# Four runs of edges per partition instead of eight, in a graph-network and mixture-of-experts kernel

## The chip, the cores and the metric

The kernel runs on one core of one Trainium2 chip. The metric is device time in microseconds (us), the median of several executions. A profile is one further execution, recorded instruction by instruction. The core's engines are TensorE (PE, with its weight loads PEld), VectorE (DVE), ScalarE (ACT), GpSimd (POOL) and SyncE (SP); each works through its own instructions in order, and they wait for one another by semaphores. Sixteen DMA engines move data between the main memory and the on-chip memory of 128 partitions; here nearly all transfers are issued from SP's queue, and gathers and scatters by index from POOL's.

## The reference

There are 6250 nodes of 256 features and 100,000 edges of 96 features. The edges are sorted by `dst`, and most go to nodes of low number.

```python
dst = jnp.minimum((6250 * uniform ** 2.0).astype(jnp.int32), 49999)   # then sorted, src with it

# graph layer, on layernorm(x); col = dst
out1 = segment_sum(edge_attr, col, n)
cnt  = segment_sum(ones, col, n)
out2 = where(cnt > 0, segment_max(edge_attr, col, n), 0)
out3 = out1 / maximum(cnt, 1)
h = concatenate([x, out1, out2, out3, u[batch]], axis=1)              # 256 + 3*96 + 64
h = relu(h @ W1 + b1) @ W2 + b2                                       # hidden 1024
x = x + (h + layernorm_x)

# mixture of 16 experts, best 2 of each node, on layernorm(x)
logits = x @ gate_w + gate_b;  w, idx = top 2, softmax of the two
moe = sum_k w_k * (relu(x @ w1[idx_k] + b1) @ w2[idx_k] + b2)         # 256 -> 512 -> 256
x = x + layernorm(x + moe) * gamma + beta
```

All numbers are fp32.

## The kernel before, in words

**Two stages.** The first makes the sums, maxima and means of the edges of each node, runs the graph layer's two products, chooses the experts and scatters the rows to the experts' lists in main memory. The second takes those lists in blocks of 256 rows (`run_block`, PE lines L1166 and L1190), and joins, normalizes and writes the result. The change lies in the first stage.

**Nodes.** A tile is 125 nodes (`P`), a group (`GRP`) has four tiles, the first group two. There are 13 groups, taken from the last nodes to the first, so that nodes with few edges come first. For a group, `hidden` (L772, L789) and `output` (L800) are PE's products, `turn` (L763) its transposes. `residual` (L805 to L810), `stats_x` (L690), `add_b2` (L724), `choose`, `rank` and `place` (L845 to L895) are DVE's work; `send` (L899) scatters the rows.

**Edges of groups 0 and 1.** Each node's few edges lie in a window of 20 edges, which is gathered, masked, summed and maximized (`cut_window` to `mask_window`, L572 to L612). `mask_window` adds a `base`, which is zero unless the input does not fit the kernel's assumptions. Then a fallback, behind a branch, computes everything more slowly.

**Edges of the other groups.** The 95,000 edges before these lie in seven regions. Region c has 125 partitions with `RR` = 8 runs each, and every run is `JR[c]` consecutive edges: 125 x 8 x (6, 5, 5, 10, 21, 20, 28). Regions 0 to 6 serve 1, 1, 1, 2, 3, 2 and 1 groups (`GR`). Within a region the kernel goes over the positions of the runs from the last to the first, all 125 x 8 runs at once. A position's row is the running sum and the running maximum over the edges of the same node up to the run's end: the row of the position behind it, times `keep` (1 if the next edge has the same node, else 0), plus this edge; and the same with `min` of `bar` and `max`. These are the four instructions of an *edge step*, on 125 partitions x `RR` x 96 elements (L316, L317, L319, L320). The first position of a region is copied by ACT.

Positions go in chunks of up to `JS` = 2. `load_edges` (L176) loads a chunk in two DMAs (80 and 45 partitions, `halves`), with three buffers `raw`; the results go from three buffers `rw` to `rows_d` in main memory (L329), in two DMAs. One contiguous piece is a chunk's positions of one run: 2 x 96 x 4 bytes in, twice that out.

**The carry.** A run's last node may go on in the next run. `chain_runs` handles that at a region's end, in three parts. `over_runs` carries over the runs of a partition (L395, L396: `RR` - 1 pairs of instructions of 96 elements into `ct`). `over_partitions` carries over partitions, after PE's transposes. `to_runs` (L436, L438) spreads the carry to all runs with four instructions of `RR` x 96 elements and stores `ct` to `carry_d` by POOL (L440). `ct` has one buffer. `take_edges` (L730) and `take_carry` (L737) gather, for each node, its row and the carry of the next run; `join_edges` (L743, L745) combines them.

**The order of work** is written by a planner when the kernel is built. A group has 12 slots; every task is put into a slot with a cost in microseconds. The edge steps are a stream (`edge_stream`): in each slot it is advanced until a credit of `SLOT` = 4.6, less the costs of the other tasks, is used up. A stream item's cost is the number after `yield`. Before a group's `take_edges`, `edges_until(c)` advances the stream to the end of that region, whatever the credit:

```python
            if fn is take_edges:
                edges_until(args[0])
            fn(*args)
            credit -= cost
```

The last region is needed at slot 134 (`B - 10` of group 12).

Of the kernel before, what the change touches and what calls it, by code (L numbers as in the profile page):

```python
# [18 lines left out]

P = 125  # L20
PA = 80
RR = 8
GW = 2
WE = 20
WB = 5
JR = (6, 5, 5, 10, 21, 20, 28)
GR = (1, 1, 1, 2, 3, 2, 1)
JS = 2
JB = 3
KB = 250  # L30
GS = 4
# [14 lines left out]
def kernel(  # L46
# [18 lines left out]
    nc = tc.nc  # L65
    N, D = x.shape
    E, EF = edge.shape
# [3 lines left out]
    NT = N // P  # L71
# [27 lines left out]
    rows_d = dram.tile([ER, 2 * EF], F32, name="rows_d")  # L99
# [199 lines left out]
    def steps():  # L299

        for i, (c, s, n) in enumerate(chunks):
            e0, J = REG[c]
            if s + n == J:
                mark_runs(c)
                yield 1.5, False, None
            raw, prev = raws.pop(i), prevs.pop(c, None)
            rw = EP_["rw"].tile([P, RR, JS, 2 * EF], F32, name="rw")
            bcast = [P, RR, EF]
            for j in reversed(range(n)):
                x_j, su, mx = raw[:, :, j, :], rw[:, :, j, 0:EF], rw[:, :, j, EF:]  # L310
                if prev is None:
                    nc.scalar.copy(su, x_j)
                    nc.scalar.copy(mx, x_j)
                    prev = x_j, x_j
                else:
                    nc.vector.tensor_tensor(su, prev[0], keep[c][:, :, s + j, None].to_broadcast(bcast), op=OP.mult)  # L316
                    nc.vector.tensor_tensor(mx, prev[1], bar[c][:, :, s + j, None].to_broadcast(bcast), op=OP.min)  # L317
                    yield 1.9, False, None
                    nc.vector.tensor_tensor(su, su, x_j, op=OP.add)  # L319
                    nc.vector.tensor_tensor(mx, mx, x_j, op=OP.max)  # L320
                    prev = su, mx
                    if j:
                        yield 1.9, True, None
            prevs[c] = prev
            if i + JB < len(chunks):
                load_edges(i + JB)
            to = rows_of(c).rearrange("(p r j) f -> p r j f", p=P, j=J)
            for o, i_ in halves(to[:, :, s:s + n], rw[:, :, :n]):
                nc.sync.dma_start(o.rearrange("p r j f -> p r (j f)"), i_.rearrange("p r j f -> p r (j f)"))  # L329
            yield 1.9, True, c if s == 0 else None  # L330

    clock = [-1]
    told = [-1]
# [43 lines left out]

    def chain_runs(c):
        prev = prevs.pop(c)
        ct = chp.tile([P, RR, 2 * EF], F32, name="ct")  # L380
        kb, kp, kb2 = (chp.tile([P, RR], F32, name=nm) for nm in ("kbar", "kp", "kbar2"))

        def over_runs():
# [9 lines left out]
            for r in reversed(range(RR - 1)):  # L393
                to = ct[:, r, 0:EF], ct[:, r, EF:]
                nc.vector.scalar_tensor_tensor(to[0], run[0], kall[:, c, r:r + 1], prev[0][:, r, :], op0=OP.mult, op1=OP.add)  # L395
                nc.vector.scalar_tensor_tensor(to[1], run[1], kb[:, r:r + 1], prev[1][:, r, :], op0=OP.min, op1=OP.max)  # L396
# [35 lines left out]
        def to_runs():  # L432
            tmp = chp.tile([P, RR, EF], F32, name="tmp")
            for h, k, o0, o1 in ((0, kp, OP.mult, OP.add), (1, kb2, OP.min, OP.max)):
# [1 line left out]
                nc.vector.tensor_tensor(tmp, over_runs.pc[:, None, h * EF:(h + 1) * EF].to_broadcast([P, RR, EF]),  # L436
                                        k[:, :, None].to_broadcast([P, RR, EF]), op=o0)
                nc.vector.tensor_tensor(cs, cs, tmp, op=o1)  # L438
# [929 lines left out]
    def windows_of(t, n):  # L1368
# [28 lines left out]
    with tc.If(bad_v != 0):  # L1397

        NC = (KC + 1) * GS * P - 1
        space = chp.tile([P, RR, EF], F32, name="tmp").rearrange("p r f -> p (r f)")  # L1400
        et, ob = space[:, 0:EF + 1], space[:, P:P + 2 * (EF + 1)].rearrange("p (h f) -> p h f", h=2)
        far, df = space[0:1, P:2 * P], space[0:1, 3 * P:4 * P]
        dt_ = space[0:1, 4 * P:5 * P].bitcast(I32)
        dst_v = dst.rearrange("(a b) -> a b", b=P)
        for lo in range(0, N, NC):
            sums = [wk.tile([128, KC + 1, GS * P], F32, name="inT").rearrange("p k n -> p (k n)")[:EF + 1] for _ in range(2)]
# [17 lines left out]
            for n0 in range(0, min(NC, N - lo), P):  # L1424
# [11 lines left out]
        nc.sync.dma_start(base[0], rows_d[W0 * P:NT * P].rearrange("(i p) f -> p i f", p=P))  # L1436
        nc.vector.tensor_scalar(nw, cnt_f[:, W0:], 1.0, None, op0=OP.min)
        for t in range(NT - W0):
            nc.vector.tensor_scalar(base[0][:, t, :], base[0][:, t, :], nw[:, t:t + 1], None, op0=OP.mult)
    with tc.manual_schedule():  # L1440
        global_part()
        stats_x(0, 0)
# [124 lines left out]
```

## Time and profile before

| what | value |
|---|---|
| time, median of 3 runs (lowest to highest) | 1291.13 us (1291.03 to 1294.33) |
| the profiled execution's own time | 1299.43 us |
| its span, mean granted TensorE clock | 1297.6 us, 0.955 |
| busy: PE, PEld | 1113.4 us (86%), 783.4 us (60%) |
| busy: DVE, ACT, POOL | 963.4 us (74%), 612.6 us (47%), 558.8 us (43%) |
| edge steps, DVE: L316, L317, L319, L320 | 352 instructions of 125x768, 948 to 955 ns each |
| to runs, DVE: L436, L438 | 28 instructions of 125x768, 949 to 961 ns each |
| over runs, DVE: L395, L396 | 98 instructions of 125x96, 310 to 318 ns each |
| moved by DMA | 261.25 MB in 179475 packets |

The span runs from the first instruction to the last; the execution's own time has 1.8 us beside it. Busy shares are means over both stages. In the slices of the profile, each engine has one digit per fortieth of the span, its busy share in tenths. Lines with stretches give the busy microseconds of each engine in a stretch, with the number of instructions, then the granted clock, the mean busy share of the 16 DMA engines and what they moved. A line of a wait names who waited, for whom, how long in all, how often, and the longest. A timeline line gives start, duration, engine, line, operation and shapes.

### The profile page before, as it was taken

How to read it: one execution, taken by the hardware profiler on the slowest of the kernel's cores; microseconds unless marked ns; L12 is line 12 of the kernel's file. 1: busy time of each engine (PE TensorE's matmuls, PEld its weight loads, DVE VectorE, ACT ScalarE, POOL GpSimd, SP SyncE). 2: the span in 40 equal slices, each digit the busy share in tenths (PEclk: the TensorE clock that was granted, in tenths of full speed). 3: DMA queues.
4: the chain of work that ended last, by engine and by line, in shares of the span. 5: the costliest groups of instructions: out<-in, count | busy, mean ns of one | idle time of the engine just before them, and what ended most of it. 6: DMA issues, size and time to landing. Idle time of an engine off the chain costs nothing.

```text
span 1297.6 us, 16883 instructions
## 1 busy us (share of the span) xinstructions
PE 1113.4 (86%) x4637; PEld 783.4 (60%) x4637; DVE 963.4 (74%) x2754; ACT 612.6 (47%) x1449; POOL 558.8 (43%) x721
## 2 busy tenths in 40 slices
PE   2484796998789989899989999998999998989992
PEld 1252363655455554646646566886888777778881
DVE  4569787988988979999989422444377777778885
ACT  3484253662437542343424422432466666656662
POOL 4121142663347645375263333030145554545664
PEclk9897898999889998999999999998999999999996
DMA  5948785797779998898997331231677777778972
GB/s 163 209 108 234 206 242 160 204 242 208 216 222 267 252 244 228 235 255 228 274 260 237 90 95 42 66 100 50 195 229 228 231 238 252 254 228 254 280 259 73
DMA packets 179475, 261.25 MB, mean 201 GB/s; under 512 B 35915, under 2 KB 145963, under 8 KB 173729
## 3 DMA queue, kind: packets, MB, share of 16 engines
q1 hardware_dynamic: 140241, 202.23, 54.4%
q0 software_dynamic: 39008, 57.35, 16.1%
q8 instruction: 40, 0.66, 0.2%
q14 instruction: 74, 0.61, 0.2%
q10 hardware_dynamic: 112, 0.41, 0.1%
HBM read 146.70 MB, written 122.01 MB: 207 GB/s over the span
## 4 chain that ended last, share of the span: by engine, by line
PE 35%; DVE 13%; ACT 3%; DMA 3%; issue 3%; POOL 1%; POOLq 0%; SPq 0%; ACTq 0%; DVEq 0%
PE acc L1190 14%; PE acc L1166 11%; PE acc L772 5%; PE acc L800 3%; DVE yb L1089 2%; ACT yb L1091 2%; DVE rw L320 1%; DVE rw L317 1%; DVE rw L319 1%; DVE rw L316 1%; DMA xt<-in_x_dram 1%; ACT hb L1172 1%; DMA cg<-carry_d,next_i 1%; DMA xg_d<-xt,pos_i 1%; POOL xg_d L899 1%
## 5 line engine op out<-in xcount | busy, mean ns | idle before, releaser
L772 PE MATMUL acc<-inT,w1x 128*128 128x500 f32 (+1 forms) x832 | 369.0, 592 | 8.9 <-DVE xt L805 8.9
L772 PEld LDWEIGHTS acc<-inT,w1x 128*128 128x128 f32 x832 | 159.0, 199 | 169.7 <-issue 151.9
L1166 PE MATMUL acc<-xT,wt 128*128 128x256 f32 x912 | 223.2, 388 | 29.3 <-ACT hb L1172 25.7
L899 POOL DMA_INDIRECT xg_d<-xt,pos_i x100 | 134.4, 1344 | 250.2 <-DVE xt L895 119.8
L1190 PE MATMUL acc<-wt,hb 128*128 128x256 f32 x912 | 207.1, 380 | 0.0
L1166 PEld LDWEIGHTS acc<-xT,wt 128*128 128x128 f32 x912 | 169.2, 191 | 62.3 <-ACT hb L1172 38.1
L1190 PEld LDWEIGHTS acc<-wt,hb 128*128 128x128 f32 x912 | 174.1, 191 | 23.9
L800 PE MATMUL acc<-w2s,hT 128*125 128x256 f32 x800 | 186.5, 388 | 0.0
L800 PEld LDWEIGHTS acc<-w2s,hT 128*125 128x125 f32 x800 | 150.5, 193 | 23.7 <-issue 1.9
L1102 POOL DMA_INDIRECT g<-y_d,from_i x86 | 91.8, 1067 | 120.8 <-DMA y_d<-yb 90.5
L1135 POOL DMA_INDIRECT out_dram<-g,to_i x86 | 89.1, 1036 | 102.7 <-ACT hb L1172 86.5
L1091 ACT ACTIVATE yb<-yb,w_b 128x256 f32<-128x256 f32 x114 | 51.7, 501 | 154.0 <-DVE yb L1089 147.8
L495 POOL DMA_INDIRECT gb<-in_dst_dram,blk_i x50 | 74.1, 1483 | 114.2 <-issue 59.4
L1172 ACT ACTIVATE hb<-acc,wt 128x256 f32<-128x256 f32 x200 | 87.7, 464 | 49.5 <-PE acc L1166 41.0
L1089 DVE TENSOR_TENSOR yb<-acc,xe 128x512 f32<-128x512 f32 x57 | 39.4, 691 | 88.3 <-PE acc L1190 57.4
L794 ACT ACTIVATE hT<-acc,c 128x500 f32<-128x500 f32 (+1 forms) x104 | 60.1, 660 | 71.4 <-PE acc L789 71.4
L319 DVE TENSOR_TENSOR rw<-rw,raw 125x768 f32<-125x768 f32 x88 | 83.8, 953 | 0.0
L320 DVE TENSOR_TENSOR rw<-rw,raw 125x768 f32<-125x768 f32 x88 | 83.7, 951 | 0.0
L316 DVE TENSOR_TENSOR rw<-rw,keep 125x768 f32<-125x768 f32 x81 | 76.8, 948 | 5.0 <-DMA rows_d<-rw 4.9
L317 DVE TENSOR_TENSOR rw<-rw,bar 125x768 f32<-125x768 f32 x81 | 77.0, 950 | 0.0
L730 POOL DMA_INDIRECT at<-rows_d,first_i x44 | 61.6, 1399 | 34.2 <-issue 21.5
L737 POOL DMA_INDIRECT cg<-carry_d,next_i x44 | 63.2, 1437 | 25.7 <-issue 11.3
(313 smaller groups left out, 1577.9 us busy)
## 6 DMA issues: line engine op xcount, KB each, us to landing
wt<-in_wpack_dram SPq DMA_DIRECT2D x44, 1026.0 KB
rows_d<-rw SPq DMA_DIRECT2D x46, 960.0 KB
rows_d<-rw SPq DMA_DIRECT2D x46, 540.0 KB
raw<-in_edge_dram SPq DMA_DIRECT2D x46, 480.0 KB
xb<-xg_d SPq DMA_DIRECT2D x57, 263.0 KB
y_d<-yb SPq DMA_DIRECT2D x57, 256.0 KB
raw<-in_edge_dram SPq DMA_DIRECT2D x46, 270.0 KB
xt<-in_x_dram SPq DMA_DIRECT2D x12, 500.0 KB
```

The source lines that it names most:

```text
L316: nc.vector.tensor_tensor(su, prev[0], keep[c][:, :, s + j, None].to_broadcast(bcast), op=OP.mult)
L317: nc.vector.tensor_tensor(mx, prev[1], bar[c][:, :, s + j, None].to_broadcast(bcast), op=OP.min)
L319: nc.vector.tensor_tensor(su, su, x_j, op=OP.add)
L320: nc.vector.tensor_tensor(mx, mx, x_j, op=OP.max)
L772: nc.tensor.matmul(G[g]["pH"][m % 4][:, :n * P], w1x[:, k, m * 128:(m + 1) * 128], inT[:, k, :n * P], start=(k == 0), stop=False)
L800: nc.tensor.matmul(pO, G[g]["hT"][m][:, i * P:(i + 1) * P], w2s[:, m, :], start=(m == 0), stop=(m == HC - 1))
L899: d = nc.gpsimd.indirect_dma_start(out=xg_d[:, :], out_offset=IndirectOffsetOnAxis(ap=G[g]["pos"][:, i, k:k + 1], axis=0), in_=G[g]["xt"][ ...
L1102: d = nc.gpsimd.indirect_dma_start(out=g[:, h, :].bitcast(I32), out_offset=None, in_=y_d[:, :], in_offset=IndirectOffsetOnAxis(ap=BL[b]["f ...
L1135: d = nc.gpsimd.indirect_dma_start(out=out[:, :], out_offset=IndirectOffsetOnAxis(ap=BL[b]["to"][:, h:h + 1], axis=0), in_=g[:, h, :], in_ ...
L1166: nc.tensor.matmul(pB[i][:, half, :], wt[:, k * FF + m * 128:k * FF + (m + 1) * 128], xT[:, k, :], start=(k == 0), stop=(k == DC - 1))
L1172: nc.scalar.activation(hb[:, m, :], pB[i][:, half, :], AF.Relu, bias=bias)
L1190: nc.tensor.matmul(pY[:, h, :], hb[:, m, h * 128:(h + 1) * 128], wt[:, W2O + m * D:W2O + (m + 1) * D], start=(m == order[0]), stop=(m == o ...
```

## The change

A partition holds four runs per region instead of eight, and `JR` is doubled, so a region holds the same edges. An edge step has 125 x 4 x 96 elements, there are twice as many positions, and a chunk has up to four of them. The planner's costs of an edge step and of the parts of the carry are set anew, and `over_runs` yields once instead of three times. `ct` gets two buffers. Before, the zero `base` of groups 0 and 1 lay in one buffer of `ct`, which is now too small for it: group 1's lies in a buffer of `ct`, group 0's in that of `tmp`. The fallback's scratch moves to buffers of `hT`. The rest of the fallback's edits is left out here.

```diff
-RR = 8
+RR = 4
-JR = (6, 5, 5, 10, 21, 20, 28)
+JR = (12, 10, 10, 20, 42, 40, 56)
-JS = 2
+JS = 4
...
                     nc.vector.tensor_tensor(su, prev[0], keep[c][:, :, s + j, None].to_broadcast(bcast), op=OP.mult)
                     nc.vector.tensor_tensor(mx, prev[1], bar[c][:, :, s + j, None].to_broadcast(bcast), op=OP.min)
-                    yield 1.9, False, None
+                    yield 1.0, False, None
                     nc.vector.tensor_tensor(su, su, x_j, op=OP.add)
                     nc.vector.tensor_tensor(mx, mx, x_j, op=OP.max)
                     prev = su, mx
                     if j:
-                        yield 1.9, True, None
+                        yield 1.0, True, None
...
-            yield 1.9, True, c if s == 0 else None
+            yield 1.0, True, c if s == 0 else None
...
-        ct = chp.tile([P, RR, 2 * EF], F32, name="ct")
+        ct = chp.tile([P, RR, 2 * EF], F32, name="ct", bufs=2)
...
                 run = to
-                if r % 3 == 0:
-                    yield 1.8
+                if r == 0:
+                    yield 1.6
...
                 nc.vector.tensor_tensor(cs, cs, tmp, op=o1)
-                yield 1.9
+                yield 1.1
...
-        nc.vector.scalar_tensor_tensor(gi, gi, nw[:, j:j + 1], base[0][:, j, :], op0=OP.mult, op1=OP.add)
+        nc.vector.scalar_tensor_tensor(gi, gi, nw[:, j:j + 1], base[1 - g][:, i, :], op0=OP.mult, op1=OP.add)
...
-    base.append(chp.tile([P, RR, 2 * EF], F32, name="ct").rearrange("p r f -> p (r f)")[:, 0:(NT - W0) * 2 * EF]
+    base.append(chp.tile([P, RR, 2 * EF], F32, name="ct", bufs=2)[:, 0:z1 - a1])
+    base.append(chp.tile([P, RR, EF], F32, name="tmp").rearrange("p r f -> p (r f)")[:, 0:(z - a) * 2 * EF]
                 .rearrange("p (t f) -> p t f", f=2 * EF))
...
-        nc.gpsimd.memset(base[0], 0.0)
+        for t in base:
+            nc.gpsimd.memset(t, 0.0)
...
-        space = chp.tile([P, RR, EF], F32, name="tmp").rearrange("p r f -> p (r f)")
+        space, more = (htp.tile([128, GS * P], F32, name="hT")[:P] for _ in range(2))
...
```

More of the change, by code (lines that the diff above doesn't have):

```diff
@@ L1399 @@
         NC = (KC + 1) * GS * P - 1
-        space = chp.tile([P, RR, EF], F32, name="tmp").rearrange("p r f -> p (r f)")
+        space, more = (htp.tile([128, GS * P], F32, name="hT")[:P] for _ in range(2))
         et, ob = space[:, 0:EF + 1], space[:, P:P + 2 * (EF + 1)].rearrange("p (h f) -> p h f", h=2)
-        far, df = space[0:1, P:2 * P], space[0:1, 3 * P:4 * P]
-        dt_ = space[0:1, 4 * P:5 * P].bitcast(I32)
+        far, df = more[0:1, 0:P], more[0:1, P:2 * P]
+        dt_ = more[0:1, 2 * P:3 * P].bitcast(I32)
         dst_v = dst.rearrange("(a b) -> a b", b=P)
@@ L1435 @@
                     nc.sync.dma_start(cnt_f[q0 - t * P:q1 - t * P, t:t + 1], ob[q0 - lo - n0:q1 - lo - n0, 0, EF:])
-        nc.sync.dma_start(base[0], rows_d[W0 * P:NT * P].rearrange("(i p) f -> p i f", p=P))
+        for t, (t0, t1) in zip(base, ((a1, z1), (a, z))):
+            nc.sync.dma_start(t, rows_d[t0 * P:t1 * P].rearrange("(i p) f -> p i f", p=P))
         nc.vector.tensor_scalar(nw, cnt_f[:, W0:], 1.0, None, op0=OP.min)
         for t in range(NT - W0):
-            nc.vector.tensor_scalar(base[0][:, t, :], base[0][:, t, :], nw[:, t:t + 1], None, op0=OP.mult)
+            to = base[0][:, t, :] if t < z1 - a1 else base[1][:, t - (z1 - a1), :]
+            nc.vector.tensor_scalar(to, to, nw[:, t:t + 1], None, op0=OP.mult)
     with tc.manual_schedule():
```

## The prediction

> **What bounds the kernel now.** I read the page's slices first, then the busy time by stretches of 100 us, then VectorE's waits, SP's waits, and last the timeline for the step from one instruction to the next. Of the slices, the engines and the DMA engines:
>
> ```profile
> PE   2484796998789989899989999998999998989992
> DVE  4569787988988979999989422444377777778885
> DMA  5948785797779998898997331231677777778972
> ```
>
> A slice is 32 us. Edges and graph MLP fill slices 4 to 24; DVE leads from slice 8 to 21 with DMA close behind, then PE alone has nines. Stretches (PE, PEld, DVE, ACT, POOL busy, then clock, DMA share, GB/s):
>
> ```profile
> 200.00:300.00 100.00, 85.53 (x340) 51.51 (x339) 81.98 (x231) 53.58 (x131) 52.75 (x46) 0.95 0.80 217
> 300.00:400.00 100.00, 84.07 (x305) 49.06 (x305) 91.32 (x230) 38.33 (x88) 48.91 (x51) 0.91 0.80 216
> 500.00:600.00 100.00, 95.12 (x379) 58.84 (x378) 95.98 (x270) 40.07 (x85) 47.15 (x43) 0.98 0.86 236
> 600.00:700.00 100.00, 94.02 (x359) 55.30 (x359) 93.31 (x199) 38.26 (x81) 42.14 (x44) 0.98 0.94 262
> 700.00:800.00 100.00, 97.36 (x383) 59.21 (x382) 41.79 (x163) 32.52 (x64) 41.73 (x59) 1.00 0.35 95
> ```
>
> From 100 to 700 us DVE is 82 to 96% busy; what it idles is named in its waits (window 100 to 740):
>
> ```profile
> DVE at L743 <- DMA cg<-carry_d,next_i: 29.4, 17, 5.4
> DVE bsa L690 <- DMA xt<-in_x_dram: 9.7, 2, 5.0
> DVE ct L395 <- DMA carry_d<-ct: 7.7, 1, 7.7
> DVE rw L316 <- DMA rows_d<-rw: 4.9, 2, 4.3
> ```
>
> These four make 51.7 us, most of what DVE idles there, and all are transfers. The time between the first residuals (L805) of successive groups is 59 to 62 us around 300 to 490 us and 46 to 47 us after 700, where PE alone sets it. So this stage lasts as long as DVE's work plus DVE's waits, and each microsecond of either counts until about 700 us. SP mostly waits for DVE to free a buffer, so DMA bandwidth is not the first bound:
>
> ```profile
> SPq L176 <- DVE rw L320: 217.4, 24, 30.8
> ```
>
> **Part 1: the edge steps (longer).** What counts is start to start, not the mean duration, because neighbours overlap:
>
> ```profile
> 619.32 0.94 DVE L317 TENSOR_TENSOR rw<-rw,bar 125x768 f32<-125x768 f32 x1
> 620.19 0.94 DVE L319 TENSOR_TENSOR rw<-rw,raw 125x768 f32<-125x768 f32 x1
> 621.06 0.94 DVE L320 TENSOR_TENSOR rw<-rw,raw 125x768 f32<-125x768 f32 x1
> 621.93 0.94 DVE L316 TENSOR_TENSOR rw<-rw,keep 125x768 f32<-125x768 f32 x1
> ```
>
> A step is 0.869 us for 768 elements per partition. The tensor-tensor rows give the price of an element: 417 ns at 256 (L805) and 1216 ns at 1024 (L724), so 799/768 = 1.04 ns, and 384 elements less save 0.40 us. A step at 384 is then 0.469 us (69 ns fixed, as at 768 and at 1024, where L724 takes 1.14 us start to start). Positions: JR sums to 95, the first of each of 7 regions is copied by ACT, so 88 x 4 = 352 instructions now (81+7, 81+7, 88 and 88 in the rows of L316, L317, L319, L320). After: 190 - 7 = 183 positions, 732 instructions. 352 x 0.869 = 305.9 us; 732 x 0.469 = 343.3 us: **+37.4 us**. The adds still read a product two instructions back, 0.94 us earlier, and that lasts 0.55 us, so the halved step makes no stall.
>
> [...]
>
> **Part 2: the carry over runs (shorter).** `over_runs` makes RR-1 pairs of 96 elements, 0.23 us apart:
>
> ```profile
> 558.75 0.31 DVE L395 SCALAR_TENSOR_TENSOR ct<-ct,kall,rw 125x96 f32<-125x96 f32 x1
> 558.98 0.31 DVE L396 SCALAR_TENSOR_TENSOR ct<-ct,kbar,rw 125x96 f32<-125x96 f32 x1
> ```
>
> 7 pairs become 3: 8 instructions x 0.23 x 7 regions = -12.9 us. `to_runs` has four dependent instructions of 768, 0.99 us apart:
>
> ```profile
> 720.05 0.96 DVE L438 TENSOR_TENSOR ct<-ct,tmp 125x768 f32<-125x768 f32 x1
> 721.04 0.96 DVE L436 TENSOR_TENSOR tmp<-ps,kbar 125x768 f32<-125x768 f32 x1
> ```
>
> At 384: 4 x 0.40 x 7 = -11.2 us. Parts 1 and 2 together: +13.3 us of DVE work. By region the net is -0.2, -0.4, -0.4, +0.9, +4.0, +3.7, +5.9 us: nothing early, nearly all after 420 us.
>
> **Part 3: where it falls.** The stream's own costs sum to 88 x 3.8 + 7 x 12.7 = 423 before and 183 x 2.0 + 7 x 7.3 = 417 after, so the planner deals it out to the same slot 134, where `edges_until(6)` takes the rest. Following its loop with these costs and pricing what is dealt by the steps above, the work dealt from slot 132 on grows from 8.7 to 15.0 us. There PE is the bound and DVE 42% busy, so 6 us are hidden; if that cover were gone, they would cost 6 us. **Charged: +7 us.**
>
> **Part 4: two carry buffers.** The 7.7 us of L395 is `over_runs` of region 2 waiting until region 1's carry store, issued at 209.65 us, has left `ct` at 221.4. With two buffers nobody waits: **-7.7 us** (nothing on DVE runs meanwhile, and PE stands too, for 9.8 us until 224.5). The store shrinks from 750 to 375 KB, and POOL's carry gathers waited 8.0, 2.1 and 1.3 us behind the stores of regions 1 to 3. But the join waits (29.4) also come from POOL issuing 16 gathers a group at about 1.5 us each, which is unchanged. Between nothing and -7.4 us (the joins at 287 to 296 us), I take **-3 us**, nearer to nothing since POOL's issue remains.
>
> **Part 5: larger transfers.** Loads and stores stay 49 chunks, so SP issues as many. Pieces double, 768 to 1536 bytes in and 1536 to 3072 out. In the trace's packet records the median packet takes 36 ns at 768 bytes, 65 at 1536 and 122 at 3076 (second stage): per pair 72 to 65 and 130 to 122. With 23,750 pairs each way that is (7+8) x 23,750 / 16 = 22 us of all DMA engines, about 4 points of share in a stage at 0.80 to 0.94. That is no gain by itself, since SP waits on DVE, but 14.6 us of DVE's idle time (xt and rows_d) comes from a crowded queue. Between 0 and -14.6, and up to +4 if longer packets hold back the small gathers, I take **-5 us**, a third.
>
> **At nothing:** two memsets of 768 and 384 in place of one of 1152 (1.05 us on POOL at 1.9 us, its first gather is at 13 us); `mask_window` with another base, same 125x192 shape; the window sums now lent from `ct` and `tmp` are read by 105 us, before region 0's carry (127 us); ACT's copies are halved with ACT at 38 to 54%; the fallback is not taken. Each is under 1 us if its cover is gone.
>
> **The sum:** +7 - 7.7 - 3 - 5 = -8.7, say -8 us on the profiled 1299.4 us (span 1297.6 plus 1.8). That execution is 8.3 us over the median of the runs, 1291.1. I take the difference to the median: **1283 us**.
>
> **Rivals.**
> - *The fixed cost grows (slower).* All hangs on the step at 384, which no row shows. Each 10 ns is 7.3 us; the sum is zero at 0.480 us and slower by over 0.3% from 0.486. At 0.50 it is 1306 us. For it: at 96 elements the pitch of L395 holds 0.13 us of fixed time, not 0.07 (at that, 1327 us). Against: that form reads a per-partition scalar, and tensor-tensor has 69 ns at 768 and at 1024. 0.25.
> - *Nothing (within 0.3%).* The 7.7 us go, but POOL's issue sets the joins and transfers stay as late, or pieces do not grow and the change does not do what it says: +7 - 7.7, 1290 us. For: POOL's gathers are serial. 0.18.
> - *DMA was the bound (far faster).* Share 0.94 at 600 to 700 and 80 of 125 partitions going in one half and 45 in the other leave some engines fuller than the mean. If most of the 51.7 us of waits went (say 30 beside the +7): 1268 us. Against: SP waits 217 us for DVE. 0.12.
> - *The forecast*, 1275 to 1291 us: 0.45.
>
> **Numbers.** About 0.3% (4 us) is what this kernel's runs can tell from no change. Faster by more: 0.42 of the forecast's 0.45 plus 0.12 = 0.54; same 0.20; slower 0.26. The range leaves out the longest tails on both sides: 1269 (DMA case) to 1306 (step at 0.50).
>
> **What would show it.** Right: L316 to L320 with x183 or so, 0.55 us mean and 0.47 us start to start; L395 at 21 instructions; no wait of L395 on carry_d; DMA share 3 to 8 points lower from 400 to 700; first residuals of groups 2 to 5 earlier by 8 to 15 us, and part of it given back by group 10. Wrong: a step above 0.48 us, join waits (L743) as long as before, or a new wait of DVE on raw or on PE's `ps` transposes at a region's end.

## The result, and the profile after

The changed kernel takes 1297.36 us (median of 20 executions, 1288.12 to 1303.69), the kernel before 1289.56 us beside it on the same chip (20, 1285.34 to 1294.42). The ratio is 1.0056, 95% interval 1.0041 to 1.0071: some 7 us slower, where 8 us less were forecast. The ratios in this document leave out executions more than 1.5% above the fastest of their kernel. The profiled execution took 1303.69 us with a span of 1301.9 us.

The slices of the changed kernel, PE, DVE and DMA:

```profile
PE   2483699988998779889989699998999999999992
DVE  5569789979997959999999631354448888888885
DMA  5948786695787876797988512122377888888882
```

DMA is lower than before in most slices of the edge stage, and PE has a 6 in slice 22 (counted from 0; from 716 us), where it had a nine. The stretches (PE, PEld, DVE, ACT, POOL busy, clock, DMA share, GB/s):

```profile
200.00:300.00 100.00, 94.40 (x372) 57.81 (x371) 85.85 (x295) 53.22 (x136) 56.02 (x45) 0.97 0.73 212
300.00:400.00 100.00, 91.08 (x336) 52.84 (x335) 94.22 (x311) 44.87 (x105) 57.61 (x57) 0.96 0.79 223
500.00:600.00 100.00, 90.04 (x341) 53.09 (x340) 96.34 (x317) 37.82 (x82) 38.84 (x41) 0.95 0.81 229
600.00:700.00 100.00, 96.18 (x379) 58.07 (x379) 95.92 (x277) 39.33 (x82) 45.04 (x48) 1.00 0.90 257
700.00:800.00 100.00, 88.71 (x328) 52.10 (x327) 49.71 (x179) 28.74 (x57) 31.86 (x43) 0.93 0.44 122
```

From 200 to 400 us PE gets more done than before (94.40 and 91.08 us busy instead of 85.53 and 84.07). From 700 to 800 it gets less done (328 matmuls instead of 383, at a clock of 0.93 instead of 1.00). VectorE's waits, window 100 to 740, and the longest of SP's:

```profile
DVE at L743 <- DMA cg<-carry_d,next_i: 33.9, 13, 7.7
DVE bsa L690 <- DMA xt<-in_x_dram: 5.7, 3, 2.1
DVE rw L316 <- DMA rows_d<-rw: 5.5, 2, 2.8
DVE tmp L436 <- PE ps L430: 4.0, 2, 3.1
SPq L176 <- DVE rw L316: 232.4, 25, 24.4
```

L395's wait for `carry_d` is gone. The joins (L743) wait longer, not shorter. This one wait scatters, though: in a second profile of each kernel it was 13.1 us before and 28.9 after. The steps themselves, on the timeline (start, duration):

```profile
618.45 0.55 DVE L316 TENSOR_TENSOR rw<-rw,keep 125x384 f32<-125x384 f32 x1
618.92 0.55 DVE L317 TENSOR_TENSOR rw<-rw,bar 125x384 f32<-125x384 f32 x1
619.39 0.55 DVE L319 TENSOR_TENSOR rw<-rw,raw 125x384 f32<-125x384 f32 x1
619.86 0.55 DVE L320 TENSOR_TENSOR rw<-rw,raw 125x384 f32<-125x384 f32 x1
...
730.88 0.31 DVE L395 SCALAR_TENSOR_TENSOR ct<-ct,kall,rw 125x96 f32<-125x96 f32 x1
731.11 0.31 DVE L396 SCALAR_TENSOR_TENSOR ct<-ct,kbar,rw 125x96 f32<-125x96 f32 x1
...
735.51 0.56 DVE L438 TENSOR_TENSOR ct<-ct,tmp 125x384 f32<-125x384 f32 x1
736.11 0.56 DVE L436 TENSOR_TENSOR tmp<-ps,kbar 125x384 f32<-125x384 f32 x1
```

The edge instructions are 0.469 us apart, the forecast figure.

**Where the time went.** The first residual (L805) of each group marks how far the stage is. The table gives microseconds between marks in one profile of each kernel: group 0 to 1, 1 to 6, 6 to 10, 10 to 12, then when the last residual starts (the length of the graph stage, called the stage below). The profiles of the experiments are in it too. Each entry is one execution, and two profiles of the same kernel differ by up to 6 us in the last column.

| kernel | 0 to 1 | 1 to 6 | 6 to 10 | 10 to 12 | last residual |
|---|---|---|---|---|---|
| before; again | 76; 77 | 308; 307 | 211; 211 | 92; 92 | 803; 806 |
| after; again | 81; 81 | 305; 304 | 213; 210 | 105; 104 | 822; 816 |
| before_end | 75 | 307 | 203 | 109 | 812 |
| before_split | 76 | 322 | 216 | 93 | 823 |
| before_lean | 77 | 305 | 212 | 93 | 807 |
| before_js1 | 78 | 311 | 220 | 105 | 833 |
| after_end | 83 | 304 | 219 | 96 | 820 |
| after_092 | 85 | 293 | 227 | 90 | 814 |
| after_break | 81 | 300 | 212 | 103 | 813 |
| after_ct1 | 83 | 300 | 211 | 102 | 814 |
| after_js2 | 76 | 297 | 210 | 105 | 808 |
| after_js2_end | 77 | 301 | 218 | 99 | 814 |
| after_lean | 81 | 299 | 207 | 105 | 811 |
| after_js2_lean | 77 | 296 | 207 | 108 | 807 |
| after_lean_end | 82 | 291 | 218 | 95 | 805 |
| after_r6 | 82 | 305 | 221 | 97 | 821 |
| mixed | 81 | 303 | 216 | 92 | 811 |
| mixed_12 | 73 | 307 | 219 | 92 | 810 |

The changed kernel loses about 5 us at the start, gains 3 from group 1 to 6, and loses 12 to 13 at the end. The 3 are what is left of some 16 gained up to group 5 (231 us instead of 246 from group 1 to 5), after group 5 to 6 took 75 us instead of 62. At both ends TensorE stands behind VectorE. At the start, its waits from 100 to 185 us, first of before, then of after:

```profile
PE ps L404 <- DVE kp L387: 10.3, 1, 10.3
PE pg L520 <- DVE rp L513: 4.8, 1, 4.8
```

```profile
PE ps L404 <- DVE kp L387: 19.7, 1, 19.7
PE pg L520 <- DVE rp L513: 9.5, 1, 9.5
```

L404 transposes region 0's carry. Before, eight matmuls of L772 (110.6 to 116.4 us) stand ahead of it in PE's program; after, it stands ahead of them, since the stream's parts have other costs. VectorE also reaches the carry 4.6 us later (L404 starts at 131.3 instead of 126.7). The order alone does not cost the 5 us, however. The kernel `after_js2` below is the changed one with two positions per load instead of four. It has the same order and the same wait at L404, and takes 76 us from group 0 to 1; what is shorter there is the wait at L520:

```profile
PE ps L404 <- DVE kp L387: 19.7, 1, 19.7
PE pg L520 <- DVE rp L513: 6.6, 1, 6.6
```

At the end, the stretch 720 to 740 us, before and after:

```profile
720.00:740.00 20.00, 20.00 (x74) 9.51 (x72) 7.78 (x32) 8.36 (x15) 10.61 (x11) 1.00 0.35 90
```

```profile
720.00:740.00 20.00, 12.66 (x25) 6.10 (x26) 15.47 (x48) 2.16 (x7) 0.61 (x1) 0.67 0.70 189
```

VectorE still has region 6's last edge steps and its carry to do, PE stands behind them (4.4 us at L404, 1.1 at L406, 1.7 at L430, 2.6 and 1.4 behind residuals, 11.2 in all from 705 to 740), and the clock is 0.67: 25 matmuls in 20 us instead of 74. From the first residual of group 10 to that of group 12, PE is idle for 11.3 us instead of 2.6, and the clock is 0.94 instead of 1.00. The low clock came together with the gaps; no run shows what lowers it.

The timed difference (7 us) is smaller than that of these profiles (about 14). Their second stages, from the last residual to the end of the span, are 495 and 495 us before and 480 and 486 after; over all rows they are 480 to 499 us, with kernels of both layouts at both ends. What sets that was not found, so half of the loss in the profiles does not show in the time, and no run says why.

### The profile page after: what moved, and what is told of

Same layout as the page of the kernel before. It is cut to its first block, busy times and chain, and to the rows that moved or that the text cites. A ratio compares the mean times of both kernels' runs of the same rounds, so it can differ in the third digit from the quotient of the medians.

```text
span 1301.9 us, 17210 instructions
## 1 busy us (share of the span) xinstructions
PE 1121.9 (86%) x4637; PEld 790.0 (61%) x4637; DVE 974.7 (75%) x3078; ACT 607.4 (47%) x1449; POOL 554.0 (43%) x722
## 4 chain that ended last, share of the span: by engine, by line
PE 41%; DVE 24%; DMA 13%; issue 6%; ACT 5%; POOL 5%; SPq 1%; POOLq 0%; ACTq 0%; DVEq 0%
PE acc L1190 14%; PE acc L1166 10%; PE acc L772 8%; PE acc L800 5%; DMA rows_d<-rw 4%; DMA xt<-in_x_dram 3%; DVE rw L317 3%; DVE rw L320 3%; DMA cg<-carry_d,next_i 3%; DVE rw L319 3%; DMA xg_d<-xt,pos_i 2%; DVE rw L316 2%; POOL gb L495 2%; DVE yb L1089 2%; ACT yb L1091 2%
## 5 line engine op out<-in xcount | busy, mean ns | idle before, releaser
L772 PE MATMUL acc<-inT,w1x 128*128 128x500 f32 (+1 forms) x832 | 368.6, 591 | 4.9 <-DVE xt L805 4.7
L772 PEld LDWEIGHTS acc<-inT,w1x 128*128 128x128 f32 x832 | 159.5, 200 | 165.9 <-issue 150.1
L899 POOL DMA_INDIRECT xg_d<-xt,pos_i x100 | 127.6, 1276 | 264.9 <-DVE xt L895 151.2
L800 PE MATMUL acc<-w2s,hT 128*125 128x256 f32 x800 | 191.1, 395 | 0.0
L800 PEld LDWEIGHTS acc<-w2s,hT 128*125 128x125 f32 x800 | 154.3, 198 | 24.1 <-issue 1.2
L316 DVE TENSOR_TENSOR rw<-rw,keep 125x384 f32<-125x384 f32 x176 | 97.0, 551 | 5.5 <-DMA rows_d<-rw 5.5
L320 DVE TENSOR_TENSOR rw<-rw,raw 125x384 f32<-125x384 f32 x183 | 100.9, 552 | 0.0
L319 DVE TENSOR_TENSOR rw<-rw,raw 125x384 f32<-125x384 f32 x183 | 100.8, 551 | 0.0
L317 DVE TENSOR_TENSOR rw<-rw,bar 125x384 f32<-125x384 f32 x176 | 97.1, 552 | 0.0
L730 POOL DMA_INDIRECT at<-rows_d,first_i x44 | 68.0, 1546 | 59.8 <-issue 40.1
L764 ACT COPY inT<-pT 128x500 f32<-128x500 f32 (+1 forms) x65 | 36.1, 555 | 86.0 <-PE pT L763 86.0
```

Source lines behind the costliest of these rows:

```text
L772: nc.tensor.matmul(G[g]["pH"][m % 4][:, :n * P], w1x[:, k, m * 128:(m + 1) * 128], inT[:, k, :n * P], start=(k == 0), stop=False)
L800: nc.tensor.matmul(pO, G[g]["hT"][m][:, i * P:(i + 1) * P], w2s[:, m, :], start=(m == 0), stop=(m == HC - 1))
L899: d = nc.gpsimd.indirect_dma_start(out=xg_d[:, :], out_offset=IndirectOffsetOnAxis(ap=G[g]["pos"][:, i, k:k + 1], axis=0), in_=G[g]["xt"][ ...
```

## The experiments

Kernels timed together ran on one chip, with the kernel before beside them. Ratios are to it, with 95% intervals.

**The end.** The theory after the first result was that the loss is the backlog at slot 134. `after_again` is the changed kernel unchanged.

> The changed kernel once more, for a second profile. In the first one the graph stage ended 18.6 us later than before (first block product L1166 at 823.7 instead of 805.1 us), while the median time is only some 7 us over before: part of the 18.6 us should be a chance event of that one execution, namely the gather of 10.5 us on POOL at 451 us. Theory 'end of the stream' (the edge steps that the planner deals from slot 132 on delay the residuals and PE's in-order transposes): 1.005 to 1.007 of before; groups 4 and 5 again 5 to 9 us earlier than before, L1166 first at about 812 to 816 us, and the step from group 10 to group 11 again 57 to 60 us instead of 46. Rival 'extra work everywhere': the loss is spread evenly over groups 6 to 12, and the step from group 10 to 11 was chance.

The ratio was 1.0064 (1.0029 to 1.0100): the loss stands. Its profile has the same stalls, group 5 to 6 76 us and group 10 to 11 58. The forecast that the long POOL gather was chance was wrong: it took 10.3 us here.

```diff
+            step = 0.92 if c == len(JR) - 1 else 1.0      # after_end; before_end: 2.15 instead of 1.9
-                    yield 1.0, False, None
+                    yield step, False, None                # and so the two other yields
```

> The changed kernel with one planner cost altered: an edge step of the last region costs 0.92 instead of 1.0, so the planner deals the same steps some slots earlier and only the carry is left for slot 134. No instruction is added or removed. Theory 'end of the stream': the step from group 10 to 11 falls from 59 to about 48 us, and the kernel gets 6 to 10 us faster, 1287 to 1291 us where before is 1289.6 (ratio 0.998 to 1.001). Rival 'extra work everywhere': VectorE has the same work before the last group either way; the time stays within 2 us of the changed kernel (ratio 1.004 to 1.007).

0.9994 (0.9954 to 1.0033). Over all twelve executions the medians give 1.0045, so this proves no gain. The profile is clearer: group 10 to 12 falls to 96 us, group 6 to 10 rises to 219, and the stage (820 us) is no shorter.

> The kernel before with one planner cost altered: an edge step of the last region costs 2.15 instead of 1.9, so that about as much of its work as in the changed kernel is left for slot 134 (13 us instead of 6). No instruction is added or removed. Theory 'end of the stream': 6 to 10 us slower than before (ratio 1.005 to 1.008), with the step from group 10 to 11 at 55 to 60 us instead of 46. Rival 'extra work everywhere': no change beyond 2 us (ratio 0.999 to 1.001).

1.0056 (1.0018 to 1.0095). In the kernel before, a backlog made in the same way costs 17 us in groups 10 to 12 and gives 8 back in 6 to 10. PE shows much the same there as in the changed kernel: 14.5 us idle and a clock of 0.94 between the residuals of groups 10 and 12.

**More and smaller instructions.** Each edge instruction of the kernel before is cut in two:

```diff
-                    nc.vector.tensor_tensor(su, su, x_j, op=OP.add)
+                    for q in (slice(0, RR // 2), slice(RR // 2, RR)):
+                        nc.vector.tensor_tensor(su[:, q], su[:, q], x_j[:, q], op=OP.add)
...
```

> The kernel before with each of the four instructions of an edge step cut into two halves of four runs: 704 instructions of 125x384 instead of 352 of 125x768, and nothing else. It adds the fixed cost alone: 352 x 0.069 = 24.3 us of VectorE. If VectorE's work sets the graph stage up to the last groups, as the prediction took it: 18 to 26 us slower (ratio 1.014 to 1.020), the last of it at the end of the stream, since the planner's costs are unchanged. Rival 'waits, not work, set the stage': under 8 us (ratio under 1.006).

1.0091 (1.0055 to 1.0126), about 12 us for 24 us of added work, below the 18 to 26 expected; the stage of its profile is 17 to 20 us longer. In the time, added work is paid for at about half its price (7 to 16 us by the interval).

**All steps dealt out faster.** `after_092` has `yield 0.92` in place of all three `yield 1.0`.

> The changed kernel with every edge step counted at 0.92 instead of 1.0 in the list of work (two instructions take 0.94 us on VectorE), so that each slot deals out a little more of the stream; no instruction is added or removed. Theory (the loss sits in two places: the lump of edge work dealt at slot 134, and POOL's gather of region 4's rows, which is held for 10 us while VectorE runs edge steps without a break): both go, group 10 to 11 takes 46 to 50 us instead of 59 and group 5 to 6 takes 62 to 66 instead of 74, no POOL gather over 5 us near 450 us, ratio to the kernel before 0.985 to 0.995. Rival (the longer carry and edge work itself costs the time, the order only moves it): ratio 1.000 to 1.006, the time lost at one group comes back at others.

1.0069 (1.0024 to 1.0115), just above the rival's range. Both lumps go (group 5 to 6 62 us, group 10 to 11 44), and groups 6 to 10 take 227 us instead of 213. The theory that the loss is two lumps fell here. Moved work seems to be paid for where it lands: VectorE is 94% busy in groups 6 to 10 here, and 95 to 97% in the kernels before and after.

**The held gather.** In the changed kernel POOL's first gather of region 4's rows takes 10 us. Eleven more gathers stand behind it on POOL, and the joins wait. POOL's timeline, and VectorE's at the moment the gather ends (L845 is the first instruction there that is no edge step):

```profile
450.54 10.47 POOL L730 DMA_INDIRECT at<-rows_d,first_i  x1 [3.35 <-issue]
461.32 1.21 POOL L730 DMA_INDIRECT at<-rows_d,first_i  x1 [0.30 <-issue]
```

```profile
459.35 0.56 DVE L320 TENSOR_TENSOR rw<-rw,raw 125x384 f32<-125x384 f32 x1
459.82 0.23 DVE L845 TENSOR_TENSOR lg<-pg,xt 125x64 f32<-125x64 f32 x1
```

```diff
+                    if c == 5 and (s + j) % 2 == 0:
+                        nc.vector.max(sm.tile([P, 8], F32, name="brk", bufs=1), b2b[:, 0:16])
```

> The changed kernel with one small VectorE instruction (a MAX8 over 16 numbers, some 0.2 us, about 4 us in all, its result used by nothing) behind every second position of region 5, whose edge steps are what VectorE runs while POOL's gather of region 4's rows is held. Theory (the gather is held by VectorE's unbroken two-input instructions): the first gather of L730 at about 450 us takes 1 to 4 us instead of 10, the waits for cg after it shrink from 14.6 us to under 6, group 5 to 6 takes 64 to 68 us instead of 74, and the time is 1 to 8 us below that of the changed kernel (ratio to before 0.999 to 1.005) although work was added. Rival (the gather waits for DMA queues that are full, or for the rows): it still takes 9 to 11 us, and the time rises by 0 to 4 us (ratio 1.005 to 1.010).

The gathers with a break after every eight edge instructions, and the breaks (in this kernel the lines behind the edit are numbered two higher):

```profile
446.50 4.11 POOL L732 DMA_INDIRECT at<-rows_d,first_i  x1 [6.11 <-DMA rows_d<-rw]
450.91 3.49 POOL L732 DMA_INDIRECT at<-rows_d,first_i  x1 [0.30 <-issue]
454.70 1.20 POOL L497 DMA_INDIRECT gb<-in_dst_dram,blk_i  x1 [0.30 <-DVE V L851]
```

```profile
449.41 0.17 DVE L322 MAX8 brk<-b2b 125x8 f32<-125x16 f32 x1
...
453.24 0.17 DVE L322 MAX8 brk<-b2b 125x8 f32<-125x16 f32 x1
```

The hold is VectorE's: each gather ends 1.2 us, its usual length, after the first instruction that breaks the run of edge steps (450.61 after 449.41, 454.40 after 453.24; without breaks 461.01 after 459.82). But the time did not fall (1.0105, 1.0048 to 1.0162), the joins still wait 28.6 us, and group 5 to 6 takes 76 us. So the hold is real, and shortening it (4.11 and 3.49 us for the first two gathers instead of 10.47 and 1.21) did not shorten the time. How VectorE holds a gather is not shown. Here the hold lasted over a run of some 20 instructions (450.54 to 459.82 us, 0.469 us apart). It does not always come: in `after_js2` gathers got through an equally unbroken run in about 1.5 us. What decides it was not found.

```profile
446.64 1.46 POOL L730 DMA_INDIRECT at<-rows_d,first_i  x1 [0.64 <-issue]
448.40 1.54 POOL L730 DMA_INDIRECT at<-rows_d,first_i  x1 [0.30 <-issue]
```

**One carry buffer.** `bufs=2` is taken from `ct`.

> The changed kernel with one carry buffer instead of two. Theory (the prediction's part 4): L395's wait for the carry store comes back, 7 to 9 us in all, half or more of it on the path, ratio to before 1.009 to 1.014. Rival (those waits only moved to other waits that end at the same time): ratio 1.004 to 1.007, as the changed kernel itself.

1.0105 (1.0054 to 1.0156), an interval that overlaps the changed kernel's. In the profile L395 has no wait at all, and the stage is as long as with two buffers. So the second buffer did not take the 7.7 us away. Region 1's store is issued at 201 us here, 198 with two buffers and 210 before, is half as large (375 instead of 750 KB), and region 2's `over_runs` starts at 221 us in both one-buffer kernels, in the kernel before only after its wait of 7.7 us. By 221 us the earlier and smaller store is out.

**Two positions per load.** `JS = 2`, `JB = 6`: pieces as long as before the change, half the size of a transfer.

> The changed kernel with two positions of each run per load and store and six loads ahead instead of four positions and three ahead: the same bytes in flight, pieces of 768 and 1536 bytes as before, twice as many transfers issued and one more carry of the edge values between tiles. Theory (the larger pieces are worth about 5 us, as the prediction charged): ratio to before 1.007 to 1.012. Rival (the transfers are hidden anyway: DMA engines are 70 to 90% busy and nothing waits for their rate): ratio 1.003 to 1.007, as the changed kernel itself.

1.0052 (1.0009 to 1.0094), the rival's figure: the longer pieces bring nothing that can be measured in the time. The profile has the shortest stage of the four-run layout with all its work (808 us), with 76 us at the start and 65 from group 5 to 6, and still has 105 at the end. The same holds for the two other kernels with two positions per load (`after_js2_end`, `after_js2_lean`): 77 us at the start, 65 and 67 from group 5 to 6, and a stage 5 to 14 us shorter than with four positions (808 against 822 and 816, 814 against 820, 807 against 811). Their joins wait 15 to 20 us instead of 29 to 34, and their loads of `x` 13 to 20 us instead of 4 to 6. So in these pairs the loss at the start and from group 5 to 6 goes with the four positions per load. Whether the length of the pieces or the size of the transfer does it stays open, since both are halved. (From group 5 to 6 the loss is also missing in `after_092` and `after_lean_end`, which have four positions but deal the steps out otherwise.) None of the pairs differs in the time (1.0056 and 1.0052, 0.9994 and 1.0014, 0.9990 and 0.9974).

**A second profile of before.**

> The kernel before, unchanged, for a second profile of it: the graph stage (to the last L805) was 803.1 us in its first profile, and 821.6, 815.6, 814.5 and 812.7 us in four profiles of the changed kernel and of variants of it that left this stage's length nearly alone. If the difference is of the kernels, it lies between 799 and 807 us again; if the first profile was a lucky one, above 810 us.

Its stage took 806 us: the difference is of the kernels.

**Both edits together.** `after_js2_end` has after_js2's and after_end's.

> The changed kernel with two edits: two positions per load and store and six loads ahead (as in after_js2), and region 6's edge steps counted at 0.92 instead of 1.0 in the list of work (as in after_end); no instruction of VectorE is added or removed. Theory (the change gains 8 us of graph stage by group 5, larger pieces give it back at group 5 to 6 because the last store of region 4 lands later, and the lump of edge work dealt at slot 134 costs 12 us more at group 10 to 11): both losses go, group 5 to 6 takes 62 to 66 us, group 10 to 11 takes 46 to 50 us, the graph stage ends at 793 to 801 us, ratio to the kernel before 0.991 to 0.998. Rival (VectorE's 13 us of added work has to be paid somewhere): the graph stage ends at 806 to 816 us, ratio 1.001 to 1.007.

1.0014 (0.9975 to 1.0053), stage 814 us: the rival. The end falls from 105 to 99 us, and groups 6 to 10 rise from 210 to 218.

**Less VectorE work.**

```diff
-                    nc.vector.tensor_tensor(mx, prev[1], bar[c][:, :, s + j, None].to_broadcast(bcast), op=OP.min)
+                    if (s + j) % 7:
+                        nc.vector.tensor_tensor(mx, prev[1], bar[c][:, :, s + j, None].to_broadcast(bcast), op=OP.min)
+                    else:
+                        mx = prev[1]
...
```

> The changed kernel without the cut of the running maximum at the starts of runs (L317) at every seventh position: 29 instructions of 0.469 us, 13.6 us of VectorE's work, spread over the stream, so as much as the change added. The maximum leaves these cuts out. Theory (the added work is largely hidden or paid for by the carry over runs; the losses are two lumps and the later stores): a third to two thirds of it shows, 4 to 9 us below the changed kernel, and group 5 to 6 and group 10 to 11 still take over 68 and 54 us. Rival (VectorE's work alone sets the graph stage): 12 to 15 us below the changed kernel, ratio to before 0.994 to 0.997, spread evenly over groups 1 to 11.

0.9990 (0.9952 to 1.0028), 0.0066 to 0.0074 below the changed kernel's ratios: about 9 us for 13.6 us of work, as much as the whole timed loss, though the intervals are wide. As the theory had it, the two stalls stay (group 5 to 6 74 us, 10 to 12 105).

> The kernel before without the cut of the running maximum (L317) at every seventh position: 15 instructions of 0.869 us, 13.0 us of VectorE's work, spread over the stream. The maximum leaves these cuts out. Theory (VectorE's work in the graph stage is paid for in both kernels, at 0.5 to 0.8 us for each us): 6 to 10 us less than the kernel before, graph stage 796 to 800 us, ratio 0.992 to 0.9955. Rival (the kernel before had room, and only the changed kernel lies on VectorE's bound, as the prediction's 6 us hidden would have it): 0 to 4 us less, ratio 0.997 to 1.000.

0.9979 (0.9937 to 1.0021), stage 807 us, no shorter than the 803 and 806 of the kernel before. This is the rival's figure, though the interval reaches into the theory's range. More work there costs half its price (before_split) and less brings little, as if VectorE stood just at the bound; that is not shown.

> The changed kernel with two positions per load and store and six loads ahead, and without the cut of the running maximum at every seventh position (29 instructions of 0.469 us, 13.6 us). The maximum leaves these cuts out. Theory (two separate losses, the added VectorE work and the late stores of the large tiles): they add up, the graph stage ends at 796 to 803 us, ratio to the kernel before 0.991 to 0.997. Rival (smaller tiles bring nothing, or the same wait is gained twice): graph stage 807 to 813 us, ratio 0.998 to 1.001, as after_lean.

0.9974 (0.9949 to 0.9999), stage 807 us, the same as after_js2. In the time the two edits seem to add up, in the profile they do not; undecided.

**Shorter pieces still**, in the kernel before: `JS = 1`, `JB = 6`.

> The kernel before with one position of each run per load and store and six loads ahead instead of two positions and three: pieces of 384 and 768 bytes instead of 768 and 1536, the same bytes in flight, twice as many transfers of half the size; VectorE's work is the same. Theory (the length of the pieces is worth nothing here, a tile of half the size is ready and stored sooner): ratio 0.996 to 1.002, the DMA engines' busy share higher. Rival (the prediction's part 5, longer pieces are worth about 5 us, so shorter ones cost as much or more): ratio 1.004 to 1.015, with longer waits for rw and raw.

1.0166 (1.0130 to 1.0202): the theory fell. Pieces of 384 and 768 bytes cost 22 us. In the profile it is the wait for the loads of `x` that grew:

```profile
DVE bsa L690 <- DMA xt<-in_x_dram: 41.7, 8, 15.2
```

That wait was 9.7 us. So piece length, or the number of transfers (both changed), has a price when loads go from 768 to 384 bytes, and none that shows in the time from 1536 to 768 (after_js2).

**Less work and a spread end.**

> The changed kernel with both edits of after_lean (13.6 us of VectorE work left out: the maximum is not cut at run starts at every seventh position) and after_end (region 6's steps counted at 0.92). From group 6 to the end of the graph stage the kernel before takes 313 us, the changed kernel 325 to 329, after_end 326, after_lean 322. Theory (the added edge steps of regions 4 to 6 fall due in groups 6 to 11, where VectorE is busy 96% of the time; moved forward they cost there, left in a lump they stall TensorE at the end; only less work and a spread end together restore it): 313 to 318 us, ratio 0.993 to 0.998. Rival (something else of the change costs 11 us there, such as the larger transfers): 321 to 326 us, ratio 0.998 to 1.002.

0.9950 (0.9920 to 0.9979), as the theory's time. Its profile does not agree with the theory's 313 to 318 us from group 6 on: it took 323, of which 218 in groups 6 to 10. It gains in groups 1 to 6 instead (291 us).

**Regions in both layouts.** `RS` holds the runs per partition of each region:

```diff
-RR = 4
-JR = (12, 10, 10, 20, 42, 40, 56)
+RR = 8
+RS = (4, 4, 4, 8, 8, 8, 8)            # mixed; mixed_12: (8, 4, 4, 8, 8, 8, 8)
+JR = (12, 10, 10, 10, 21, 20, 28)     # mixed; mixed_12: (6, 10, 10, 10, 21, 20, 28)
```

Sizes and transfers follow by region, `ct` has one buffer, and the index arithmetic of the later groups has a few instructions more.

> A kernel with the layout of the change for regions 0 to 2 only (four runs per partition, 12, 10 and 10 long, four positions per load) and that of before for regions 3 to 6 (eight runs, 10, 21, 20 and 28 long, two positions per load); one carry buffer; three or four small VectorE instructions more in the arithmetic of the gathers' indices of the later groups. VectorE's work is that of before less about 1 us, plus about 1 us for the indices. Theory (the change gains 6 to 8 us by group 4 or 5 since L395's wait for the carry store goes, and loses it from group 6 on through longer edge steps in regions 4 to 6): group 5 at 417 to 424 us, from group 6 to the end 312 to 317 us, graph stage 794 to 800 us, ratio to the kernel before 0.991 to 0.997. Rival (the early gain is given back at the joins of group 6 whatever the layout): graph stage 802 to 807 us, ratio 0.998 to 1.002.

0.9938 (0.9903 to 0.9974): faster than the kernel before, and so than the changed one. The end is back at 92 us. The expected gain by group 5 is small (428 before, 426 here), and the profiled execution, at 1300.21 us, was 7.6 us over its median, with a stage of 811 us. So its time is shown, and what makes it faster is not.

> The layout of the change in regions 1 and 2 alone, that of before in region 0 and in regions 3 to 6. In the changed kernel and in mixed, TensorE's transposition of region 0's carry stands ahead of eight matmuls of L772 instead of behind them and waits 19.7 us for VectorE instead of 10.3; group 0 to 1 takes 81 us instead of 75. Theory (that loss is region 0's alone): group 0 to 1 takes 74 to 76 us again, group 10 to 12 takes 92, the time is 2 to 6 us below mixed (ratio to the kernel before 0.989 to 0.994). Rival (the start is made up for at the next joins): the same time as mixed, ratio 0.993 to 0.997.

0.9983 (0.9967 to 1.0000), and group 0 to 1 takes 73 us: the start's loss comes with region 0's layout. (Region 0 has its old order on PE and its old transfers here, so this does not tell the one from the other.) On another chip than `mixed`, with times that scatter less; which of the two is better stays open.

`after_r6` is the change in all regions but the last: `RS = (4, 4, 4, 4, 4, 4, 8)`.

> The layout of the change in regions 0 to 5 and that of before in region 6 alone (eight runs of 28, two positions per load); one carry buffer; a few small VectorE instructions more in the indices of the last groups. Region 6's VectorE work falls by about 6 us. In the profiles so far the kernel before takes 75 us from group 0 to 1, 308 from 1 to 6, 211 from 6 to 10 and 92 from 10 to 12; the changed kernel takes 81, 305, 212 and 105. Theory (the largest loss is region 6's backlog at the end): 81, 300 to 306, 206 to 213 and 92 to 96 us, ratio to the kernel before 0.995 to 1.000. Rival (the end is lost to something else, such as the carry or the larger pieces of the earlier regions): 100 to 106 us for group 10 to 12, ratio 1.002 to 1.006.

1.0086 (1.0061 to 1.0111): the rival's side, though the end fell to 97 us. Groups 6 to 10 rose to 221, with waits for `x` of 4.8 and 5.0 us. It differs from `mixed` in regions 3 to 5 alone, whose part of the added work, by the prediction's own account, is 0.9 + 4.0 + 3.7 = 8.6 us; the ratios lie 0.015 apart (on different chips), so more than this work. What makes up the rest is open.

## Why the prediction was wrong

**Part 1 and part 2 were right.** The step is 0.469 us, L316 to L320 come 183 times, a mean of 551 to 552 ns, the pairs of L395 and L396 0.23 us apart. So VectorE has the 13.3 us more to do in the graph stage (over the whole execution its busy time rose by 11.3 us). The rival "the fixed cost grows" is out.

**Part 3 failed: the hidden 6 us.** The work at the end was put at nothing under a PE that "is the bound". PE went through its program in order, and what it waited for there was this work (11.2 us from 705 to 740 us). The end costs 12 to 13 us, twice the 6 us that were to be paid even without cover: between the residuals of groups 10 and 12 PE is idle for 8.7 us more, and the rest goes with the clock of 0.94 instead of 1.00. before_end makes this loss in the kernel before. Dealing the work out earlier empties the end but does not shorten the stage (after_end, after_092, after_js2_end): it costs in groups 6 to 10, where VectorE has little room, what it saves at the end. What helped was less work (after_lean); mixed, which adds hardly any, is faster too, but its profile does not show why. That the stream's planned costs sum to nearly the same (423 and 417) said nothing about this, since its real work grew by 13.3 us.

**The premise of the sum** was that each microsecond of VectorE's work or waits counts until about 700 us. The runs do not bear it out: 24 us more work cost 12 us (before_split), 13 us less brought some 3, not clear of nothing (before_lean), and the second profile of before has 13.1 us instead of 29.4 at L743 with a stage 3 us longer.

**Left out: the start.** The new costs put L404 ahead of eight matmuls, and group 0 to 1 takes 5 us more. No step of the prediction looked there. It goes with region 0's layout (mixed_12), and not with the order alone, since two positions per load undo it with the order unchanged (after_js2).

**Part 4, the 7.7 us:** the wait went, as forecast, and groups 2 to 5 came 6, 1, 8 and 9 us earlier than in the first profile of before, and 12, 7, 14 and 16 us earlier in the second pair of profiles (8 to 15 were forecast). The cause was not the second buffer (after_ct1). The account also stopped at the wait: of the time gained by group 5 nothing is left at group 6 in the first pair and 2 us in the second (493 and 491 us; 490 and 493 before).

**Part 4, the 3 us at the joins:** not found. L743 waited 33.9 and 28.9 us instead of 29.4 and 13.1, behind gathers that POOL issues later. The rival "nothing" had named POOL's serial issue. Of the three waits of POOL that this step counted, the view puts the longest (8.0 us) down to a gather of rows and not to the carry store.

**Part 5, larger transfers, 5 us:** the share fell as forecast (0.86 to 0.81 and 0.94 to 0.90), the wait for `xt` from 9.7 to 5.7 us, and no time follows from it: after_js2, with the old pieces, is not slower. In the profiles the stage is 5 to 14 us longer with four positions per load than with two, most of it at the start and from group 5 to 6; the step had this at a gain. The price of a loaded packet of 1536 bytes was taken from stores, 65 ns; it took 76 in the changed kernel, so two of 768 bytes (36 each) were no dearer.

**The sum.** By place the profiles give +5 (start), -3 (groups 1 to 6), +1 (6 to 10) and +12 to +13 (end), some +15 us, against a forecast of -8. The sum had start and end at nothing, which leaves some 6 us of the difference for the middle, where gains of some 16 us (no wait for the carry store, shorter carries) were lost again, most of them from group 5 to 6. The profile of after_js2, with two positions per load, has 0 at the start, -12 in the middle and +13 at the end: there the gains are kept and the loss at the end remains. The timed loss is about half of the 15; the other half is in the second stage, and open.

The rival that ended slower had another mechanism (a dearer step). Two of the signs named as wrong came: join waits as long as before (33.9 us at L743), and a wait of DVE on PE's `ps` transposes (4.0 us at L436), which was not new but had been 1.5.

## What to carry to other kernels

Work counted as hidden under another engine is only hidden if that engine does not wait for it: look up, in its program order, which instruction of it depends on the work, and what stands behind that one. Where a planner deals out work by costs, a change of costs moves instructions on every queue, so follow each queue past the change at its first and its last use, and not only where the work grows. Where an engine is some 95% busy, as VectorE is in groups 6 to 10 here, moving its work there was no remedy (`after_092`: 14 us more there, 15 us less at the end, 1.0069). Keeping the dearer layout out of the regions where it adds work gave the fastest kernel here (`mixed`, 0.9938), though what makes it faster is not shown.

## What had not been expected of the hardware

A gather issued by POOL, 1.2 to 1.5 us as a rule, took 9.5 to 10.5 us in five profiles (after, after_again, after_end, after_ct1, after_r6) and 6.5 us in one gather of the kernel before, while VectorE ran two-input steps without a break, and ended 1.2 us after the first other instruction; in other profiles it passed beside such a run in 1.5 us. Packets of 384 bytes took 22 ns in the median (before_js1), of 768 bytes 36, of 1536 bytes loaded 76 in the changed kernel (69 to 86 in kernels with the same pieces) and of 3072 bytes stored 121: from 768 to 1536 bytes a load gained nothing per byte in these medians.
